# Layer 3's diagonal weights in early-free memory, its first image normalised on ScalarE, and the small group-norm operations of the scans moved off VectorE

## The chip, the cores and the metric

The kernel runs on one core of a Trainium2 chip. The metric is the device time of one execution in microseconds (us). The engines are called PE (TensorE, matmuls), DVE (VectorE), ACT (ScalarE), POOL (GpSimd) and SP (SyncE, which here only issues DMAs). Each engine has a program of its own and runs it in order. Semaphores let one engine wait for another.

## The reference

An input of 16 images with 192 channels of 64 x 64 pixels passes through four layers. Each one normalises its input by groups (32 groups of 6 channels), applies something and adds the result to its input:

```python
def _gn(v, G=32, eps=1e-5):
    g = v.reshape(B_, G, C_ // G, H_, W_)
    m = jnp.mean(g, axis=(2, 3, 4), keepdims=True)
    s = jnp.var(g, axis=(2, 3, 4), keepdims=True)
    return ((g - m) / jnp.sqrt(s + eps)).reshape(v.shape)

x = x + layer0(_gn(x))   # a small tanh network for each channel, a likelihood
x = x + layer1(_gn(x))   # a 192x960 product over each pixel and its 4 neighbours
x = x + layer2(_gn(x))   # selective scans over the image in 4 directions:
                         #   h = exp(d*A)*h + (d*u)*B ;  y = sum over 16 states of h*C
x = x + layer3(_gn(x))   # depthwise convolution (29 taps in all), 192x192 product,
                         #   batch norm over all images, clip to 0..6
```

## The kernel before

**Tiling.** Two images make a pair: 2 x 192 channels are NT = 3 tiles of 128 partitions (`j`) with 4096 pixels each. There are 8 pairs (`npair`, called "images" in the code). A pair goes through `front` (layers 0 and 1 and the projections of layer 2), `scans` (the recurrences of layer 2) and `layer3`. At the very end the batch norm of all pairs is applied.

**Scans.** `scans` runs 768 steps for a pair: 3 tiles x 4 directions x 4 stretches of 1024 pixels x 16 states. In one step DVE multiplies (`pbt<-du,pbt`, 1.21 us) and scans (`h<-dA,state,pbt`, 2.35 us), ACT computes `dA` and copies the last column into `state`, POOL multiplies `h` by `cb` (2.35 us), and PE spreads B over the partitions (`pbt`) and sums over states (`ysum`). SP loads a row of C for each step into `cb`, 512 KB. Every operation in here goes through `_Engines(tc, True)`: it is kept in the order of the program on its engine. Buffers run ahead: `dA` by three steps, `pbt` and `cb` by two, and `ysum` follows four steps behind (`LATE`) with eight buffers for `h`.

**The front of the next pair** is a generator that is advanced a little in each step of the scans, so layers 0 and 1 of pair i+1 run beside the scans of pair i. Only the front of the first pair runs alone, and there the operations are not kept in order. `group_norm` (line 357) is called three times in each front, and once more in the last 13 steps of the scans, for tiles 0 and 1 only (`gn0`, line 1048), because these two tiles are finished early. It aggregates the statistics (`mv`), copies the means, sums them over a group with small matmuls (`gn_sum`, a `yield` after each tile), forms `d2`, sums again, and takes the power -0.5 on POOL (`rstd`). All but the matmuls and the power are on DVE.

**Layer 3** (line 1107) is written without a kept order: a planner that orders instructions by the time at which it thinks them ready places them, some of them between the scans' own. Tile 0 (`xps[0]`) and tile 1 come back from DRAM, tile 2 is still in memory (`X`). Tile 0 is normalised on DVE in four pieces with `gm0, rstd0` from `gn0`. Then `group_norm` runs for all three tiles and tiles 1 and 2 are normalised. For each of 4 stretches `c` and each tile `j`, 8 taps are matmuls with diagonal matrices on PE (`l_p<-xp,diag`, line 1164), 8 taps are ACT products (`l_m`, line 1155) summed by POOL (`l_g`, line 1159, 7 additions), POOL's sum is added on PE with the identity (line 1176), and 13 taps run on DVE (line 1182). Then `pw` mixes the channels (`zp`, line 1196), ACT copies (`z`, line 1203) and DVE takes statistics (line 1204).

**Memory.** Pools lie one above the other, and the pools of layer 3 start at the place of those of `scans`. A tile in space that the scans used waits for the last reader there. In KB for each partition, counted from that place, the scans have `Xt` 0 to 16, `xc` to 20, eight `h` to 52, `dA` to 64, `cb` to 80, `state` to 80.2, and above that what the front uses. Layer 3 has its small tiles to 0.8, `z` to 8.8, `diag` 8.8 to 20.8, `pw` to 24.3, `l_g`, `l_m` and `l_y` to 68.3, an empty tile `gap` of `GAP` = 16 KB to 84.3, and then `xp0` and `xp1`, 19.1 KB each. `gap` puts the two images above the scans' own tiles: their space is free as soon as the front has ended.

Of the kernel before, what the change touches and what calls it, by code (L numbers as in the profile page):

```python
# [11 lines left out]
F32 = mybir.dt.float32  # L12
BF16 = mybir.dt.bfloat16
AF = mybir.ActivationFunctionType
ALU = mybir.AluOpType
# [7 lines left out]
P = 128  # L23
C = 192
NT = 3
# [24 lines left out]
PE_TAPS = 8  # L50
GP_TAPS = 8

GAP = 16


class _InOrder:


    def __init__(self, tc, engine):
        self._tc, self._engine = tc, engine  # L60
# [10 lines left out]
class _Engines:  # L71
# [3 lines left out]
    def __init__(self, tc, in_order):  # L75
        nc = tc.nc
        of = (lambda e: _InOrder(tc, e)) if in_order else (lambda e: e)
        self.pe, self.act, self.dve = of(nc.tensor), of(nc.scalar), of(nc.vector)
        self.gps, self.sp = of(nc.gpsimd), of(nc.sync)
        self._later = []  # L80
        self._in_order, self._table = in_order, None

    def later(self, call):

        if self._in_order:
            self._later.append(call)
        else:
            call()
# [4 lines left out]
        self._later.clear()  # L93

    def table(self, *names):
        if self._in_order and self._table not in names:
            self._table = names[0]
            self.act.preload_act_table_set(names[0])

# [7 lines left out]
def conv_preact_kernel(ctx: ExitStack, tc: tile.TileContext, a: dict):  # L107
    nc = tc.nc
    x_in = a["x"]
    out = a["out"]  # L110
    npair = x_in.shape[0]

    def row_tiles(ap):
        return ap.rearrange("(j p) l -> p j l", p=P)
# [4 lines left out]
    x3_d = dram.tile([npair, NT, P, S, S], F32, name="x3_d")  # L119
# [4 lines left out]
    diag_d = dram.tile([P, NT, PE_TAPS, P], F32, name="diag_d")  # L124
# [80 lines left out]
    with tc.tile_pool(name="prep", bufs=1) as prep, tc.tile_pool(  # L205
        name="prep_ps", bufs=2, space=PSUM
# [88 lines left out]
        for j in range(NT):  # L295
            diag = prep.tile([P, PE_TAPS, P], F32, name="diag", tag="diag", bufs=2)
# [43 lines left out]
    def normalise(eng, o, v, gm, rstd, j):  # L340
        eng.tensor_scalar(o, v, gm[:, j : j + 1], rstd[:, j : j + 1], ALU.subtract, ALU.mult)

    def on_scalar(E, o, v, less, rstd, j):

        E.act.activation(o, v, AF.Identity, bias=less[:, j : j + 1])
        E.act.activation(o, o, AF.Copy, scale=rstd[:, j : j + 1])
# [12 lines left out]
    def group_norm(E, st, stat, ps, gm, rstd, tiles=range(NT)):  # L359


        m = len(tiles)
        mv = stat.tile([P, NT, 2], F32, name="mv", tag="mv")
        mean = stat.tile([P, NT], F32, name="mean", tag="mean")
        d2 = stat.tile([P, NT], F32, name="d2", tag="d2")
        half = stat.tile([P, NT], F32, name="half", tag="half")
        E.dve.memset(half, -0.5)
        for j in tiles:
            E.dve.bn_aggr(mv[:, j, :], st[:, j, :, :].rearrange("p c s -> p (c s)"))
        mean, d2, half, mv = mean[:, :m], d2[:, :m], half[:, :m], mv[:, :m, :]  # L370
        gm, rstd = gm[:, :m], rstd[:, :m]
        E.dve.tensor_copy(mean, mv[:, :, 0])

        def mean_of(src):
            s = ps("gn_sum")
            for jo in tiles:
                into = [x for x in INTO[jo] if x[1] in tiles]
                for n, (b, ji) in enumerate(into):
                    E.pe.matmul(
                        s[:, jo : jo + 1],  # L380
                        grp[:, b, :],
                        src[:, ji : ji + 1],
                        start=(n == 0),
                        stop=(n == len(into) - 1),
                    )
                yield
            return s[:, :m]

        s = yield from mean_of(mean)
        E.dve.tensor_scalar(gm, s, 1.0 / 6.0, None, ALU.mult)  # L390
        E.dve.tensor_tensor(d2, mean, gm, ALU.subtract)
        E.dve.tensor_tensor(d2, d2, d2, ALU.mult)
        E.dve.tensor_tensor(d2, d2, mv[:, :, 1], ALU.add)
        s = yield from mean_of(d2)
        E.dve.tensor_scalar(d2, s, 1.0 / 6.0, 1e-5, ALU.mult, ALU.add)
        E.gps.tensor_tensor(rstd, d2, half, ALU.pow)


# [45 lines left out]
    def layer0(i, E, ps, deep, st, gm, rstd):  # L444
        with tc.tile_pool(name="l0w", bufs=1) as w_, tc.tile_pool(name="l0x", bufs=3) as xk, tc.tile_pool(
            name="l0", bufs=2
        ) as wk, tc.tile_pool(name="l0t", bufs=1) as tk:
            less = w_.tile([P, NT], F32, name="less")
            E.dve.tensor_scalar(less, gm, -1.0, None, ALU.mult)
            wm = w_.tile([P, NG, P + GR], F32, name="wms")  # L450
            wt = w_.tile([GR, NG, 2 * P], F32, name="wts")
            E.sp.dma_start(out=wm, in_=wm_d)
# [265 lines left out]
    def project(o, E, ps):  # L718

        with tc.tile_pool(name="pjw", bufs=1) as w_, tc.tile_pool(name="pjx", bufs=2) as xk:  # L720
            less = w_.tile([P, NT], F32, name="less")
            E.dve.tensor_scalar(less, o.gm, -1.0, None, ALU.mult)
            proj = w_.tile([P, NT, 2 * P + K * RD], F32, name="projs")
            E.sp.dma_start(out=proj, in_=a["proj"])
            xns = {}

            def load(c):
                if c < 8:
                    xns[c] = xk.tile([P, NT, 512], F32, name="pj_x")
                    for j in range(NT):  # L730
                        E.sp.dma_start(
                            out=xns[c][:, j, :],
                            in_=row_tiles(o.x2)[:, j, 512 * c : 512 * c + 512],
                        )

            load(0)
            yield
            for c in range(8):
                load(c + 1)
                xn = xns.pop(c)  # L740
                for j in range(NT):
                    on_scalar(E, xn[:, j, :], xn[:, j, :], less, o.rstd, j)
                    yield 0.36
                for to, d0, m in ((o.b, 0, P), (o.c, P, P), (o.dt, 2 * P, K * RD)):
                    p = ps("pj_p")[:m]
                    for j in range(NT):
# [103 lines left out]
    def scans(i, o, p3, st3, begun, nxt):  # L850

        E = _Engines(tc, True)
        with ExitStack() as es:

            def pool(name, bufs, **kw):
                return es.enter_context(tc.tile_pool(name=name, bufs=bufs, **kw))
# [8 lines left out]
            ps = Banks(pool("l2_ps", 1, space=PSUM), 2)  # L865
# [178 lines left out]
            fin = iter(())  # L1044
            gstep = iter(())

            gm0, rstd0 = (p3.tile([P, NT], F32, name=f"first{n}") for n in range(2))
            gn0 = group_norm(E, st3, p3, ps, gm0, rstd0, range(2))
            for s in range(total):
                t, n = divmod(s, N)  # L1050
                j, k, at, first = todo[t]
# [50 lines left out]
            E.between()  # L1102
            for _ in gn0:
                pass
            return gm0, rstd0

    def layer3(i, st3, gm0, rstd0, o_next):
        E = _Engines(tc, False)

        with tc.tile_pool(name="l3s", bufs=1) as stat, tc.tile_pool(name="l3z", bufs=2) as zk, tc.tile_pool(  # L1110
            name="l3w", bufs=1
        ) as w_, tc.tile_pool(name="l3", bufs=2) as wk, tc.tile_pool(name="l3gap", bufs=1) as gap, tc.tile_pool(
            name="l3x", bufs=1
        ) as xk, tc.tile_pool(name="l3_pt", bufs=2, space=PSUM) as pt, tc.tile_pool(
            name="l3_pz", bufs=4, space=PSUM
        ) as pz:
            gap.tile([P, GAP * 256], F32, name="gap")
            xps = [xk.tile([P, S, S], F32, name=f"xp{j}") for j in range(NT - 1)] + [X]
            for j in range(NT - 1):
                nc.sync.dma_start(out=xps[j], in_=x3_d[i, j])  # L1120
            for r in range(0, HW, 16):
                v = xps[0][:, 3 + r : 19 + r, inside]
                normalise(nc.vector, v, v, gm0, rstd0, 0)
            diag = w_.tile([P, NT, PE_TAPS, P], F32, name="diag")
            nc.sync.dma_start(out=diag, in_=diag_d)
            pw = load("pw", [P, len(BLOCKS), P], w_)
            nc.sync.dma_start(out=x3_d[i, NT - 1], in_=X)
            gm = stat.tile([P, NT], F32, name="gm")
# [4 lines left out]
            for j in range(1, NT):  # L1133
                v = xps[j][:, inside, inside]
# [10 lines left out]
            for c in range(4):  # L1145
# [3 lines left out]
                for j in range(NT):  # L1149

                    g = wk.tile([P, 1024], F32, name="l3_g")
                    for tap in TAPS[PE_TAPS:own]:
                        first = tap is TAPS[PE_TAPS]
# [6 lines left out]
                    ps = pt.tile([P, 1024], F32, name="l3_p")  # L1160
# [30 lines left out]
                for jo in range(NT):  # L1191
                    z = zk.tile([P, 1024], F32, name="z")
                    for h in range(2):
                        ps = pz.tile([P, 512], F32, name="zp", tag="ps")
# [11 lines left out]
                        out=row_tiles(z_d[i])[:, jo, 1024 * c : 1024 * c + 1024], in_=z  # L1206
# [24 lines left out]
    with tc.tile_pool(name="fin", bufs=1) as fin, tc.tile_pool(  # L1231
        name="fin_ps", bufs=1, space=PSUM
# [30 lines left out]
        ps = over_images(zs[:, :, :, 0])  # L1263
# [6 lines left out]
        ps = over_images(dev)  # L1270
# [127 lines left out]
```

## Time and profile before

| what | value |
|---|---|
| time, median of 3 runs (lowest to highest) | 27888.86 us (27888.48 to 27893.94) |
| the profiled execution's own time | 27887.51 us |
| its span, first to last instruction | 27885.6 us |
| mean granted TensorE clock | 0.912 |
| first front, alone | 0 to 1203 us |
| scans of a pair with a front beside them (7 of 8) | 2952 to 2960 us |
| scans of the last pair, no front | 2806 us |
| from the last scan of a pair to the first of the next (layer 3) | 341 to 342 us |
| after the last layer 3: batch norm and output | about 460 us |

The page of the profile gives busy shares over the whole span. Since the kernel has stages with different limits, it is read here stage by stage: the scans, and layer 3. In lines of the groups view, the number after the bar is the total busy time in us, then the mean of one instruction in ns, and after the second bar the idle time of its engine ahead of it with what ended it. In lines of the timeline the first two numbers are start and duration in us, and the bracket is the idle time of that engine just before.

### The profile page before, as it was taken

What the parts mean: (1) busy time and instruction counts of PE and PEld (TensorE: products, weight loads), DVE (VectorE), ACT (ScalarE), POOL (GpSimd) and SP (SyncE); (2) the same over time, 40 slices, a digit from 0 to 9 for tenths busy, and PEclk for the clock granted to TensorE, in tenths of its full rate; (3) what the DMA queues carried; (4) which work ended last, traced back from release to release, by engine and by line L of the source; (5) the groups of instructions that cost most, each with busy time, mean ns of one, the idle gap of its engine ahead of it and who ended that gap; (6) DMA issues with size and microseconds to landing.
All of it is one profiled execution on the core that took longest, in us unless ns stands there. A gap on an engine that the chain in (4) does not pass through costs nothing. (4 is left out here: it accounts for less than half of the span.)

```text
span 27885.6 us, 208702 instructions
## 1 busy us (share of the span) xinstructions
PE 23499.7 (84%) x57652; PEld 9648.3 (35%) x57652; DVE 24195.1 (87%) x15397; ACT 16075.9 (58%) x23023; POOL 20709.2 (74%) x10241
## 2 busy tenths in 40 slices
PE   8799978999789987999779997899878998776662
PEld 4343323333233332433334332333323333222221
DVE  0399988999899998999989998899989999899994
ACT  7388445874468643784548844587446854344442
POOL 2388877887778876888768877788777887677771
PEclk9899989999899988999889998999989999888886
DMA  4489764897468973888748976589747897367755
GB/s 101 136 225 230 212 206 141 225 223 220 152 191 226 223 223 117 224 227 219 215 124 229 225 213 193 152 227 224 221 134 208 226 222 222 110 189 193 198 164 241
DMA packets 1999218, 5471.76 MB, mean 196 GB/s; under 512 B 550440, under 2 KB 550664, under 8 KB 1977568
## 3 DMA queue, kind: packets, MB, share of 16 engines
q1 hardware_dynamic: 1773408, 4592.80, 55.6%
q0 software_dynamic: 221184, 805.40, 15.3%
q10 hardware_dynamic: 3456, 60.21, 0.5%
q8 instruction: 459, 7.52, 0.1%
q14 instruction: 711, 5.82, 0.1%
HBM read 3908.47 MB, written 340.96 MB: 152 GB/s over the span
## 5 line engine op out<-in xcount | busy, mean ns | idle before, releaser
L66 POOL TENSOR_TENSOR h<-h,cb 128x1024 f32<-128x1024 f32 x6144 | 14868.7, 2475 | 4513.4 <-ACT state L66 3628.4
L66 DVE TENSOR_TENSOR_SCAN h<-dA,state,pbt 128x1024 f32<-128x1024 f32 x4608 | 10809.3, 2346 | 722.2 <-ACT dA L66 120.6
L66 PE MATMUL ysum<-h,ident 128*128 128x512 f32 x18432 | 9462.4, 639 | 162.6 <-DMA h<-h 161.8
L66 DVE TENSOR_TENSOR pbt<-du,pbt 128x1024 f32<-128x1024 f32 x6144 | 7429.7, 1209 | 607.3 <-PE pbt L66 458.8
L66 ACT ACTIVATE dA<-delta,t_alog 128x1024 f32<-128x1024 f32 x6144 | 7034.1, 1146 | 6.5
L66 PEld LDWEIGHTS ysum<-h,ident 128*128 128x128 f32 x18432 | 3782.6, 206 | 4472.0 <-issue 3945.6
L66 ACT COPY state<-h 128x1 f32<-128x1 f32 x6144 | 1143.4, 186 | 6527.1 <-DVE h L66 6469.2
L66 PE MATMUL pbt<-bp,pick 96*128 96x512 bf16 x8192 | 2715.2, 416 | 2040.1 <-DVE h L66 1981.4
L66 DVE TENSOR_TENSOR_SCAN h<-dA,pbt 128x1024 f32<-128x1024 f32 x1536 | 3507.5, 2284 | 207.3 <-DMA h<-h 33.2
L66 PE MATMUL p<-t,wts 96*128 96x512 f32 x5376 | 2704.1, 601 | 129.9 <-ACT t L66 128.6
L66 PE MATMUL p<-m,wms 128*96 128x512 f32 (+1 forms) x5376 | 2646.4, 593 | 6.6 <-ACT lu L66 3.3
L66 PEld LDWEIGHTS <-pick 96*128 96x128 bf16 x8192 | 694.9, 101 | 4836.1 <-DVE h L66 3189.4
L66 ACT ACTIVATE t<-p,bias 96x512 f32<-96x512 f32 x2688 | 1803.6, 677 | 967.3 <-PE p L66 952.2
L1159 POOL TENSOR_TENSOR l_g<-l_g,l_m 128x1024 f32<-128x1024 f32 x672 | 1620.7, 2412 | 626.5 <-ACT l_g L1155 490.8
L66 PE MATMUL l_p<-l_xp,w1s 128*128 128x512 f32 x3920 | 1848.9, 600 | 9.1 <-POOL l_xp L66 9.0
L66 PE MATMUL pbt<-bp,pick_mix 96*128 96x512 bf16 x4096 | 1288.6, 397 | 548.9 <-DVE h L66 542.9
L66 POOL DMA_DIRECT2D h<-h x1536 | 1363.6, 888 | 495.1 <-POOL h L66 422.2
L66 PEld LDWEIGHTS p<-t,wts 96*128 96x128 f32 x5376 | 1009.7, 190 | 1277.2 <-issue 870.3
L66 ACT ACT_TABLE_LOAD x1082 | 1388.2, 1283 | 19.3
L1182 DVE SCALAR_TENSOR_TENSOR l_p<-xp,wc,l_p 128x1024 f32<-128x1024 f32 x768 | 990.4, 1290 | 246.9 <-PE l_p L1176 220.9
L66 PEld LDWEIGHTS p<-m,wms 128*96 128x96 f32 (+1 forms) x5376 | 944.1, 176 | 743.2 <-issue 359.1
L66 ACT ACTIVATE m<-m,bias,sp 96x512 f32<-96x512 f32 x1344 | 1078.0, 803 | 169.6 <-DMA m<-l_xn 164.6
(239 smaller groups left out, 18876.6 us busy)
## 6 DMA issues: line engine op xcount, KB each, us to landing
cb<-cp_d SPq DMA_DIRECT2D x2048, 512.0 KB
cb<-c_d SPq DMA_DIRECT2D x2048, 512.0 KB
h<-h POOLq DMA_DIRECT2D x1536, 512.0 KB, 7.0
cb<-cp_d SPq DMA_DIRECT2D x2048, 256.0 KB
cb<-c_d SPq DMA_DIRECT2D x2048, 256.0 KB
m<-l_xn SPq DMA_DIRECT2D x3072, 128.0 KB
bp<-bp_d SPq DMA_DIRECT2D x384, 192.0 KB
x_d<-X SPq DMA_DIRECT2D x24, 2450.0 KB
```

The lines of the kernel that those rows point to most:

```text
L66: return self._tc.keep_in_program_order(call(*args, **kw))
L1159: nc.gpsimd.tensor_tensor(g, g, m, ALU.add)
L1182: nc.vector.scalar_tensor_tensor(image(y if tap is TAPS[-1] else ps), window(j, 16 * c, 16, tap), factor(j, tap), image(ps), ALU.mult, ALU ...
```

## The change

Three things change.

1. `diag` moves from the pool `l3w` to the pool `l3x` of the two images, ahead of them, and `GAP` grows from 16 to 25. Its DMA is issued between those of `xp0` and `xp1`.
2. The first image of layer 3 (`xps[0]`) is normalised with `on_scalar` (two ACT operations for each of four pieces) in place of one DVE operation for each. `first_norm` hands over the negated mean for it (`less0`).
3. In a group norm whose operations are kept in order (`aside`), the copy of the means, the scaling of the first sum and that of the second go to ACT, and the constant, the three operations on `d2` and the added 1e-5 go to POOL. A `yield` is added ahead of the second sum. The negated means of layer 0 and of the projections (`less`) go to ACT.

```diff
-GAP = 16
+GAP = 25
@@ group_norm
-        E.dve.memset(half, -0.5)
+        aside = E.in_order
+        small = E.gps if aside else E.dve
+        small.memset(half, -0.5)
...
-        E.dve.tensor_copy(mean, mv[:, :, 0])
+        if aside:
+            E.act.copy(mean, mv[:, :, 0])
+        else:
+            E.dve.tensor_copy(mean, mv[:, :, 0])
...
         s = yield from mean_of(mean)
-        E.dve.tensor_scalar(gm, s, 1.0 / 6.0, None, ALU.mult)
-        E.dve.tensor_tensor(d2, mean, gm, ALU.subtract)
-        E.dve.tensor_tensor(d2, d2, d2, ALU.mult)
-        E.dve.tensor_tensor(d2, d2, mv[:, :, 1], ALU.add)
+        if aside:
+            E.act.activation(gm, s, AF.Copy, scale=1.0 / 6.0)
+        else:
+            E.dve.tensor_scalar(gm, s, 1.0 / 6.0, None, ALU.mult)
+        small.tensor_tensor(d2, mean, gm, ALU.subtract)
+        small.tensor_tensor(d2, d2, d2, ALU.mult)
+        small.tensor_tensor(d2, d2, mv[:, :, 1], ALU.add)
+        yield
         s = yield from mean_of(d2)
-        E.dve.tensor_scalar(d2, s, 1.0 / 6.0, 1e-5, ALU.mult, ALU.add)
+        if aside:
+            E.act.activation(d2, s, AF.Copy, scale=1.0 / 6.0)
+            E.gps.tensor_scalar(d2, d2, 1e-5, None, ALU.add)
+        else:
+            E.dve.tensor_scalar(d2, s, 1.0 / 6.0, 1e-5, ALU.mult, ALU.add)
         E.gps.tensor_tensor(rstd, d2, half, ALU.pow)
@@ layer0, and the same with o.gm in project
-            E.dve.tensor_scalar(less, gm, -1.0, None, ALU.mult)
+            E.act.activation(less, gm, AF.Copy, scale=-1.0)
@@ scans
-            gn0 = group_norm(E, st3, p3, ps, gm0, rstd0, range(2))
+            def first_norm():
+                yield from group_norm(E, st3, p3, ps, gm0, rstd0, range(2))
+                E.act.activation(less0[:, 0:1], gm0[:, 0:1], AF.Copy, scale=-1.0)
+
+            gn0 = first_norm()
@@ layer3
             gap.tile([P, GAP * 256], F32, name="gap")
+            diag = xk.tile([P, NT, PE_TAPS, P], F32, name="diag")
             xps = [xk.tile([P, S, S], F32, name=f"xp{j}") for j in range(NT - 1)] + [X]
-            for j in range(NT - 1):
-                nc.sync.dma_start(out=xps[j], in_=x3_d[i, j])
+            nc.sync.dma_start(out=xps[0], in_=x3_d[i, 0])
+            nc.sync.dma_start(out=diag, in_=diag_d)
+            nc.sync.dma_start(out=xps[1], in_=x3_d[i, 1])
             for r in range(0, HW, 16):
                 v = xps[0][:, 3 + r : 19 + r, inside]
-                normalise(nc.vector, v, v, gm0, rstd0, 0)
-            diag = w_.tile([P, NT, PE_TAPS, P], F32, name="diag")
-            nc.sync.dma_start(out=diag, in_=diag_d)
+                on_scalar(E, v, v, less0, rstd0, 0)
```

`on_scalar` was there before, for layer 0 and the projections:

```python
    def on_scalar(E, o, v, less, rstd, j):
        E.act.activation(o, v, AF.Identity, bias=less[:, j : j + 1])
        E.act.activation(o, o, AF.Copy, scale=rstd[:, j : j + 1])
```

More of the change, by code (lines that the diff above doesn't have):

```diff
@@ L80, in __init__ @@
         self._later = []
-        self._in_order, self._table = in_order, None
+        self.in_order, self._table = in_order, None
     def later(self, call):
-        if self._in_order:
+        if self.in_order:
             self._later.append(call)
@@ L95, in table @@
     def table(self, *names):
-        if self._in_order and self._table not in names:
+        if self.in_order and self._table not in names:
             self._table = names[0]
@@ L721, in project @@
             less = w_.tile([P, NT], F32, name="less")
-            E.dve.tensor_scalar(less, o.gm, -1.0, None, ALU.mult)
+            E.act.activation(less, o.gm, AF.Copy, scale=-1.0)
             proj = w_.tile([P, NT, 2 * P + K * RD], F32, name="projs")
@@ L1045, in scans @@
             gstep = iter(())
-            gm0, rstd0 = (p3.tile([P, NT], F32, name=f"first{n}") for n in range(2))
-            gn0 = group_norm(E, st3, p3, ps, gm0, rstd0, range(2))
+            gm0, rstd0, less0 = (p3.tile([P, NT], F32, name=f"first{n}") for n in range(3))
+            def first_norm():
+                yield from group_norm(E, st3, p3, ps, gm0, rstd0, range(2))
+                E.act.activation(less0[:, 0:1], gm0[:, 0:1], AF.Copy, scale=-1.0)
+            gn0 = first_norm()
             for s in range(total):
@@ L1104, in scans, with layer3 @@
                 pass
-            return gm0, rstd0
-    def layer3(i, st3, gm0, rstd0, o_next):
+            return less0, rstd0
+    def layer3(i, st3, less0, rstd0, o_next):
         E = _Engines(tc, False)
```

## The prediction

> **What bounds the kernel now.** First the windows view, over the first pair's scans and the start of its layer 3; then the groups of DVE.
>
> ```profile
> 1203.00:4157.00 2954.00, 2623.60 (x6544) 1082.08 (x6544) 2766.29 (x1696) 1869.89 (x2751) 2376.82 (x1188) 0.93 0.82 220
> 4164.25:4192.36 28.11, 7.42 (x30) 6.85 (x31) 20.45 (x22) 8.85 (x8) 21.89 (x8) 0.55 0.45 162
> 4192.36:4208.84 16.48, 16.48 (x40) 6.39 (x40) 4.74 (x2) 8.98 (x8) 11.37 (x5) 0.93 0.00 0
> ```
>
> After the length come PE, PEld, DVE, ACT, POOL. In the scans DVE is busy for 2766 of 2954 us, and much of its rest is a tenth of a us between dependent instructions: DVE bounds them. ACT has 1084 us free, POOL 577. Behind the last scan no engine is bound: PE works 7.4 of 28.1 us, then DVE 4.7 of 16.5.
>
> ```profile
> L66 DVE TENSOR_TENSOR_SCAN h<-dA,state,pbt 128x1024 f32<-128x1024 f32 x4608 | 10809.3, 2346 | 722.2 <-ACT dA L66 120.6 <-DMA h<-h 114.7 <-DVE pbt L66 87.3
> L341 DVE TENSOR_SCALAR xp<-xp,first,first 128x1024 f32<-128x1024 f32 x32 | 58.5, 1830 | 8.7 <-POOL first L66 8.7
> L66 DVE COPY mean<-mv 128x3 f32<-128x3 f32 (+1 forms) x29 | 56.5, 1949 | 1.0
> L66 DVE TENSOR_TENSOR d<-d,mv 128x3 f32<-128x3 f32 (+1 forms) x29 | 49.9, 1722 | 1.0
> L66 DVE TENSOR_TENSOR d<-d 128x3 f32<-128x3 f32 (+1 forms) x29 | 10.9, 376 | 1.0
> L66 DVE TENSOR_SCALAR d<-gn_sum 128x3 f32<-128x3 f32 (+1 forms) x29 | 4.4, 151 | 17.4 <-PE gn_sum L66 17.4
> ```
>
> A copy of three columns takes 1.95 us, about as long as a scan of 1024. The timeline says why:
>
> ```profile
> 4100.39 2.34 POOL L66 TENSOR_TENSOR h<-h,cb 128x1024 f32<-128x1024 f32 x1 [1.22 <-PE ysum L66]
> 4100.65 2.11 DVE L66 COPY mean<-mv 128x2 f32<-128x2 f32 x1
> 4110.22 2.35 POOL L66 TENSOR_TENSOR h<-h,cb 128x1024 f32<-128x1024 f32 x1 [1.23 <-ACT state L66]
> 4110.39 2.19 DVE L66 TENSOR_TENSOR d<-d,mv 128x2 f32<-128x2 f32 x1
> ```
>
> Both end with POOL's multiplication: DVE stands still for it, with the next product and scan behind. Last, the step from scans to layer 3, in the timeline:
>
> ```profile
> 4163.22 1.03 ACT L66 COPY X<-ysum 128x1024 f32<-128x1024 f32 x1 [5.94 <-PE ysum L66]
> 4166.50 21.49 POOL L1159 TENSOR_TENSOR l_g<-l_g,l_m 128x1024 f32<-128x1024 f32 x7 [6.80 <-ACT l_m L1155]
> 4176.22 0.32 SPq L1125 DMA_DIRECT2D diag<-diag_d  x1
> 4180.90 3.12 PE L379 MATMUL gn_sum<-mean,t_grp 128*128 128x1 f32 x14 [17.71 <-DVE mean L372]
> 4191.07 15.86 PE L1164 MATMUL l_p<-xp,diag 128*128 128x512 f32 x32
> 4208.84 17.23 DVE L1182 SCALAR_TENSOR_TENSOR l_p<-xp,wc,l_p 128x1024 f32<-128x1024 f32 x13 [11.71 <-PE l_p L1176]
> ```
>
> `diag` is loaded only when DVE has read `Xt` for the last time, PE's first product starts 27 us after the last scan's sum, and DVE then waits 11.7 us for it.
>
> **What the Trainium skill says.** "SBUF — State Buffer", § Who interferes with whom: a DVE copy or tensor_scalar in a two-port mode, and a tensor_tensor with two SBUF inputs, take the port pair that GpSimd uses, and who is second is blocked for the whole instruction of the other; ACT waits for nobody. The four lines above agree, and `d<-d` at 0.16 us between POOL's work shows the bare cost. "Perfetto Trace Analysis", § Optimizing Scalar/DVE Operations: with DVE saturated, move work to Scalar, or to GpSimd with the reservation of that port. "ScalarE: Activation LUTs", § Table sets: the hidden batching unit: copy and identity are in every set; so I count no table load (1.283 us each in this trace).
>
> **The change part by part.**
>
> *Small operations.* 29 group norms run in the scans (3 x 7 and 8). Gone from DVE: copies 56.5, `d<-d,mv` 49.9, `d<-d` 10.9, `d<-mean` 8.3 + 3.2 + 3.1, `gm` 2.0 + 1.1 + 1.0, `d<-gn_sum` 4.4, `less` 1.2 + 1.0: 142.6 us, and the 17.4 us that DVE waited for PE. The constant lies inside an aggregation: 0. Added to ACT: 3 or 4 operations like the state copy (0.186 us), into a row with 37% free. Added to POOL: 5; for its small tensor_tensor the trace has 0.2 us (96x6, in the preparation), so about 1 us for each norm, where POOL has 1.2 us free in each step of 3.57. Behind a late `d2` on POOL stands the next `h`; eight buffers and PE's four steps of distance cover it. Without this cover PE, and then `pbt`, would be late by that 1 us. The added `yield` costs the front a step, beside the scans: 0.
>
> *First image.* 32 tensor_scalars, 58.5 us, and 8.7 us of waiting for `rstd0` leave DVE. ACT gets 64 operations of 1.15 us (row `l_g<-xp,wc`, 1.152): 9.2 us for each pair, in the last 7 steps, where ACT works 17.8 of 74 us (windows view, 4090 to 4164). Behind them wait `state` (then POOL's `h`) and `dA`, three steps ahead. `xp0` is ready by about 20 us after `rstd0`, before X is copied.
>
> Sum of rows: 142.6 + 17.4 + 58.5 + 8.7 = 227 us. Successive DVE instructions overlap by some 0.07 us in the timeline (220 of them: 15 us). Check by steps, from one scan's start to the next in the timeline: around a front's norm, 6.2, 6.3 and some 3.9 us fall to 4.5 (the aggregations stay), 3.6 and 3.6, about 5 us for each of 21; around the last norm 6.25, 6.36, 6.43 and three of 5.46 fall to 4.25 and 3.6, 13.3 us for each of 8: 105 + 107 = 212 us. I take **-205**, bounds -225 and -150 (a quarter eaten by waits for PE's `pbt` and the h DMA, which end 459 and 148 us of DVE's idle time in the waits view).
>
> *Early `diag`.* Layer 3's pools lose 12 KB below `gap` and gap gains 9: `l_g` comes to 12.3 to 20.3 KB, on `Xt` and `xc`; `diag` to 81.3, above the scans' 80.2, `xp0` to 93.3. So `diag` is loaded with `xp0`, at 3773 us in the first pair, 400 us earlier. Its 1.5 MB pass SP beside the `cb` loads; the two images (4.9 MB) cost DVE 2.1 + 1.2 us there, waiting for the h DMA. Added: 1.5 us x 8 = **+12** (0 to +40).
>
> PE's 32 products of the first tile (14 to 16 us) can then run from 4163, in its idle 17.7 us ahead of `gn_sum`. DVE finds them done at 4197, when it has normalised tiles 1 and 2: up to 11.7 us for each pair. Against this, `l_g` can now be written only when `Xt` has been read (4176 before). But POOL then leaves the port alone: DVE's four additions took 1.94 us where POOL was idle and 2.9 beside it, so they and the norm end some 2 us earlier; POOL then ends its first sum near 4195, and starts the second, which waits for tile 1, near 4198 (4197 before). What is late next is POOL: a sum each 19.3 us (17.0 and 2.3 waiting), against DVE's 16.8 for a tile. In the chain of waits of the last layer 3, POOL's sums lead up to the first change of `c`; there `z` stands in ACT's program behind `l_m`, PE stands behind `z`, and POOL idles 13.4 us. PE and DVE some 10 us earlier let `z` come earlier and shorten that. I take 8 us x 8 = **-64**, bounds -184 and 0 short of the rival below.
>
> Sum: 27887.5 (the profiled execution's own time) - 205 - 64 + 12 = **27630 us**. The median of the runs lies 1.4 us above that execution; I leave this out.
>
> **Rivals.**
> A. Layer 3 gains nothing, because POOL's chain from tile 1 on is the bound (the chain view of the last layer 3 speaks for it; also the case if `diag` isn't early, for it has to pass SP). 27887.5 - 205 + 12 = 27694.
> B. The first change of `c` closes wholly: 10 + 13 us x 8 = -184: 27511. For it: the chain; against: the next changes of `c` keep stalls of their own.
> C. Slower. The order in layer 3 is a planner's. If it puts the power of the norm behind all seven additions of a first sum that starts 12 us later, `rstd` comes 8 us late, all tiles behind it, and if `z` then falls behind POOL at two more changes of `c`, 2 x 13.4: 35 us for each pair, 280 in all: 27694 + 280 = 27974. It decides from 24 us for each pair, which eats the 193. For it: the 13.4 us at the first change is such a stall now. Against: the norm stands ahead of the convolution in the program.
>
> **How the numbers follow.** Forecast 0.55, A 0.26, B 0.10, C 0.09. The range of the likeliest is 27560 to 27690; A lies at its edge, B just inside the lower end that I give, C outside: **27500 to 27770**. 0.2% (56 us) is what a measurement of this kernel can tell from no change. Forecast, B and most of A are faster by more: 0.87; within: 0.05 (A with the bound of -150); slower: 0.08.
>
> **What would show it.** Scans of 2927 us with a front and 2793 without; `mean` on ACT at 0.2 us; no step above 5 us among the last 13 of the scans; `diag` issued near `xp0`; the first `l_p` of a pair within 5 us of the last `ysum`; the 11.7 us before DVE's first tap gone; 330 us between the scans in place of 341. I am wrong in the first part if POOL or PE make DVE wait in those steps, in the second if POOL's second sum starts later than 33 us behind the X copy.

## The result and the profile after

| what | before | after |
|---|---|---|
| median (lowest to highest), 4 runs each on the same chip | 27889.76 us (27888.48 to 27893.94) | 27646.29 us (27639.74 to 27651.77) |
| the profiled execution's own time | 27887.51 us | 27649.24 us |
| mean granted TensorE clock | 0.912 | 0.918 |

The ratio of after to before is 0.9912, with a 95% interval of 0.9895 to 0.993. The forecast was 27630 us. It is 16 us off, but two of its terms were off by more than that, in opposite directions. The trace, cut into stages at the first and last scan of each pair, shows it:

| stage, us | before | after | difference |
|---|---|---|---|
| first front, alone | 1203.3 | 1203.5 | +0.2 |
| scans of all 8 pairs | 23498.2 | 23259.1 | -239.1 |
| the 7 gaps between the scans of two pairs (layer 3) | 2390.2 | 2391.0 | +0.8 |
| from the last scan to the end | 793.8 | 793.9 | +0.1 |

All of the gain is in the scans. Layer 3, for which 64 us were forecast, gained nothing: 341.5 us for each pair before, 341.6 after.

The windows view of the kernel after, over the stretches that answer to those of before (columns: length, then busy us and count of PE, PEld, DVE, ACT, POOL, then clock, DMA share, GB/s):

```profile
1203.00:4120.00 2917.00, 2601.85 (x6544) 1071.65 (x6544) 2732.94 (x1662) 1882.11 (x2775) 2379.84 (x1208) 0.94 0.83 223
4126.71:4151.02 24.31, 19.56 (x56) 11.45 (x55) 16.64 (x23) 7.81 (x7) 7.96 (x5) 0.78 0.33 123
4151.02:4168.01 16.99, 8.81 (x18) 2.28 (x18) 8.80 (x3) 6.95 (x6) 16.68 (x6) 0.71 0.00 0
```

The first line is 37 us shorter, and DVE has 33 us less work in it. In the second, the way to the normalisation of tiles 1 and 2 is 3.8 us shorter and PE works 19.6 us of it instead of 7.4: the diagonal products did move forward. In the third DVE is busy for 8.80 us where it was 4.74, with the same two normalisations in it, and POOL is busy all the time.

The groups of the kernel after show where the small operations went, and at what price (total us, then mean ns):

```profile
L66 DVE TENSOR_TENSOR_SCAN h<-dA,state,pbt 128x1024 f32<-128x1024 f32 x4608 | 10809.2, 2346 | 736.2 <-ACT dA L66 106.0 <-DMA h<-h 99.4 <-DVE pbt L66 83.8
L66 POOL TENSOR_SCALAR d<-d 128x3 f32<-128x3 f32 x21 | 12.2, 581 | 0.0
L66 POOL TENSOR_TENSOR d<-d,mv 128x3 f32<-128x3 f32 x21 | 4.1, 197 | 1.6
L66 ACT COPY mean<-mv 128x3 f32<-128x3 f32 x21 | 3.7, 177 | 0.0
L345 ACT ACTIVATE xp<-xp,first 128x1024 f32<-128x1024 f32 x32 | 35.6, 1158 | 0.3
L346 ACT ACTIVATE xp<-xp,first 128x1024 f32<-128x1024 f32 x32 | 37.1, 1158 | 0.0
```

The copy of the means that took 1.95 us on DVE takes 0.177 us on ACT. The timeline of the last steps of the first pair's scans:

```profile
4076.12 0.57 DVE L66 BATCH_NORM_AGGREGATE mv<-st 128x2 f32<-128x48 f32 x2
4076.62 1.21 DVE L66 TENSOR_TENSOR pbt<-du,pbt 128x1024 f32<-128x1024 f32 x1
4077.93 2.35 DVE L66 TENSOR_TENSOR_SCAN h<-dA,state,pbt 128x1024 f32<-128x1024 f32 x1
...
4087.89 0.50 POOL L66 TENSOR_TENSOR d<-mean,first 128x2 f32<-128x2 f32 x1
4088.47 0.20 POOL L66 TENSOR_TENSOR d<-d 128x2 f32<-128x2 f32 x1
4088.75 0.20 POOL L66 TENSOR_TENSOR d<-d,mv 128x2 f32<-128x2 f32 x1
```

DVE has only the aggregation between two steps. The step with it takes 4.07 us from scan to scan and the others 3.57 to 3.67, where six steps of before took 5.46 to 6.43.

Now the step from the scans to layer 3, in the timeline of the kernel after:

```profile
4125.45 11.45 PE L1183 MATMUL l_p<-xp,diag 128*128 128x512 f32 x26
4125.65 1.03 ACT L66 COPY X<-ysum 128x1024 f32<-128x1024 f32 x1 [5.50 <-PE ysum L66]
4136.65 1.17 ACT L1174 ACTIVATE l_g<-xp,wc 128x1024 f32<-128x1024 f32 x1 [9.98 <-DVE X L66]
4139.01 7.21 POOL L1178 TENSOR_TENSOR l_g<-l_g,l_m 128x1024 f32<-128x1024 f32 x3 [16.44 <-DVE st L66]
4150.11 0.88 POOL L410 TENSOR_TENSOR rstd<-d,half 128x3 f32<-128x3 f32 x1 [3.89 <-DVE d L409]
4151.02 4.43 DVE L341 TENSOR_SCALAR xp<-xp,gm,rstd 128x4096 f32<-128x4096 f32 x1 [0.99 <-POOL rstd L410]
4155.37 4.44 DVE L341 TENSOR_SCALAR X<-X,gm,rstd 128x4096 f32<-128x4096 f32 x1
4164.49 3.46 PE L1195 MATMUL l_p<-l_g,ident 64*64 64x512 f32 x8 [6.12 <-POOL l_g L1178]
4168.01 11.89 DVE L1201 SCALAR_TENSOR_TENSOR l_p<-xp,wc,l_p 128x1024 f32<-128x1024 f32 x9 [8.19 <-PE l_p L1195]
```

PE's first product starts 0.2 us ahead of the X copy. But ACT's `l_g` waits 9.98 us for DVE's last reading of `Xt` (the name behind the arrow is `X`, the sum that reads it), POOL's first sum begins 12.3 us behind the X copy's end, is held up for `rstd` after three of its additions, and the rest of it runs beside DVE's two normalisations. These take 4.43 and 4.44 us, where they took 2.4 before, and POOL's last four additions of that sum take 13.5 us (4150.97 to 4164.49), where the first three took 7.2. DVE then still waits, 8.19 us, for PE's addition of POOL's sum.

### The profile page after: what moved, and what is told of

Its sections match the earlier page's. It is cut to its first block, busy times and chain, and to the rows that moved or that the text cites. A ratio compares the mean times of both kernels' runs of the same rounds, so it can differ in the third digit from the quotient of the medians.

```text
span 27647.5 us, 208708 instructions
## 1 busy us (share of the span) xinstructions
PE 23437.4 (85%) x57652; PEld 9614.6 (35%) x57652; DVE 23966.9 (87%) x15146; ACT 16170.9 (58%) x23198; POOL 20728.4 (75%) x10386
## 5 line engine op out<-in xcount | busy, mean ns | idle before, releaser
L66 DVE TENSOR_TENSOR pbt<-du,pbt 128x1024 f32<-128x1024 f32 x6144 | 7427.4, 1209 | 592.2 <-PE pbt L66 444.7
```

The lines of the kernel that those rows point to most:

```text
L66: return self._tc.keep_in_program_order(call(*args, **kw))
```

## The experiments

Two things were open: whether the parts of the gain add up, and what holds layer 3. Each kernel below has one time, beside the kernel before on the same chip; the last but one was timed repeatedly. Differences in the total below some 56 us are not read as such. The stage sums from the traces are finer, with a spread of up to 33 us in the sum of the eight scans between kernels that do the same in them, and of 1 to 2 us in one layer 3.

**The parts one at a time.** Small operations alone: `diag` and the first image as before.

```diff
-            diag = xk.tile([P, NT, PE_TAPS, P], F32, name="diag")
...
-                on_scalar(E, v, v, less0, rstd0, 0)
+                normalise(nc.vector, v, v, gm0, rstd0, 0)
+            diag = w_.tile([P, NT, PE_TAPS, P], F32, name="diag")
```

> Part 3 alone: small operations of the norms off VectorE, the rest as before. If a saved VectorE instruction counts at its full length in the scans (theory), the rows of before give 144 us: about 27746 us, and layer 3 stays at 341 us between the scans. If the two added yields of a front, which shift layers 0 and 1 against the 16 states of a stretch, bring the rest of what the scans gained (rival), it is 27715 us and the steps of layer 1 far from any norm are shorter.

First image alone:

```diff
-        aside = E.in_order
+        aside = False
...
-        yield
...
+            diag = w_.tile([P, NT, PE_TAPS, P], F32, name="diag")
+            nc.sync.dma_start(out=diag, in_=diag_d)
```

> Part 2 alone: the first image of layer 3 normalised on ScalarE. Theory: the rows of before, 58.5 + 8.7 us, all of it: about 27823 us, the steps of 5.46 us near the end of the scans gone, layer 3 unchanged at 341 us. Rival (ScalarE's extra 9.2 us for each pair hold up state and dA): less than 30 us, with steps above 4 us where the pieces lie.

Early `diag` alone:

```diff
-        aside = E.in_order
+        aside = False
...
-                on_scalar(E, v, v, less0, rstd0, 0)
+                normalise(nc.vector, v, v, gm0, rstd0, 0)
```

> Part 1 alone: diag in early-free memory. Theory (the head's gain is eaten by l_g, which now lies on Xt): 27890 us within 20, layer 3 at 341 us, PE's first product right behind the last sum, but POOL's first addition 19 us behind the last scan in place of 9.4. Rival (early diag is worth something, hidden in the whole change by another part): 27830 us or less.

| kernel | time, us | before beside it | difference | scans, 8 pairs | layer 3, a pair |
|---|---|---|---|---|---|
| small operations alone | 27722.26 | 27907.4 | -185 | 23332.6 | 341.3 |
| first image alone | 27838.49 | 27907.4 | -69 | 23453.3 | 340.9 |
| early `diag` alone | 27921.02 | 27907.4 | +14 | 23531.7 | 341.5 |

The first two sum to -254 us, against -243 for the whole change: as far as one time each can tell, they add, and the third adds nothing. The small operations gave 41 us more than the theory had for them. That is less than one time can tell, but it is the rival's number; the run with the `yield` alone, below, tests that rival. The early `diag` does in its own run what it does in the change (first product 6.0 us behind the last scan instead of 34), and layer 3 stays where it was. Its +14 us are below what one time can tell. The traces tell more: the two images, and here `diag` between them, are issued in the steps 667 to 676 of the first seven pairs, and the steps 660 to 720 of these take 1545.2 us in sum with the early `diag` alone and 1544.6 before. No cost of its DMA shows there.

**The space of `l_g`.** An empty tile of 12 KB below `l_g` puts it back where it lay before, above `Xt`; `gap` gives the 12 KB up, so `diag` and the images stay where the change has them.

```diff
-            gap.tile([P, GAP * 256], F32, name="gap")
+            low.tile([P, 12 * 256], F32, name="low")
+            gap.tile([P, (GAP - 12) * 256], F32, name="gap")
```

> The whole change, with an empty tile of 12 KB below l_g and gap 12 KB smaller, so that l_g, l_m and l_y lie where they lay before and diag stays early. Theory (l_g's wait for Xt eats the gain of the head): POOL's first addition 9.4 us behind the last scan, VectorE's first tap near 38 to 42 us (48.1 with the change), layer 3 at 331 to 337 us, in all 27565 to 27610 us. Rival (the order of z and l_m on ScalarE at the change of c sets layer 3, whatever the head): first tap earlier too, but layer 3 stays at 341 us: 27646 us.

27633.38 us (before beside it 27907.4: -274), layer 3 338.6 us. The tile does what it should: POOL's first addition comes 9.0 us behind the last scan instead of 19.1, and the first of the two normalisations is back at 2.41 us and the second at 3.49. DVE's first tap comes 8.7 us earlier than in the kernel after, and yet layer 3 is only 3.0 us shorter, less than the theory asked for (331 to 337 us). So the new wait on `Xt` is real and costs 3 us for each pair; it isn't what ate the rest.

**The `yield` alone**, in the kernel before:

```diff
         E.dve.tensor_tensor(d2, d2, mv[:, :, 1], ALU.add)
+        yield
         s = yield from mean_of(d2)
```

> The kernel before with the added yield alone, nothing moved off VectorE. The whole change shortened the stretch of steps 480 to 576 (layer 1, no norm in it) by 10.9 us for each pair and lengthened 48 to 96 by 4.8 and 624 to 672 by 3.7. Theory (the yields shift the front against the states): the same signs and sizes here within 2 us, the scans of a pair 0 to 5 us shorter, in all 27850 to 27900 us. Rival (it is the freed VectorE that shortens them): no stretch moves by more than 2 us.

27901.22 us, before beside it 27897.6: no difference. The three stretches did move as expected (by -9.7, +4.9 and +4.6 us for each pair), so it is the `yield` that shifts them, but the eight scans in sum didn't get shorter (23512.0 us against 23498.2): the `yield` by itself brings no gain, against the rival of the first run. Two things inside moved. The normalisation of the next tile's `xn` on DVE, 4096 columns, stood behind a run of POOL's in the kernel before; with the front one step later it doesn't. The timelines of DVE and POOL of the kernel before,

```profile
3097.69 8.48 DVE L66 TENSOR_SCALAR xn<-xn,gm,rstd 128x4096 f32<-128x4096 f32 x1
...
3096.78 7.23 POOL L66 TENSOR_TENSOR h<-h,cb 128x1024 f32<-128x1024 f32 x3
```

and of the kernel after, at the same step of the scans:

```profile
3091.88 2.39 DVE L66 TENSOR_SCALAR xn<-xn,gm,rstd 128x4096 f32<-128x4096 f32 x1
...
3090.50 4.33 POOL L66 TENSOR_SCALAR l_xp<-l_xp,fgm,frstd 128x640 f32<-128x640 f32 x1
```

8.48 us against 2.39 for the same instruction. Over all pairs the `xn` normalisations inside the scans fall from 106.3 to 68.5 us with the `yield` alone, and to 73.2 us in the kernel after. In the run with the `yield` alone this comes back as waiting: DVE's idle time that ends with POOL's `h` or `X` rises from 61.3 to 106.2 us (waits view). It does the same in the kernel after (102.5 us).

**The order of DVE's taps.** On top of `l_g` off `Xt`, the taps are kept in the order of the program instead of the planner's. In the planner's order, with `l_g` off `Xt`, three taps of tile 1 stand ahead of tile 0's last one, and the first of them waits 6.6 us for POOL's second sum.

```diff
+            V = _InOrder(tc, nc.vector)
...
-                        nc.vector.scalar_tensor_tensor(
+                        V.scalar_tensor_tensor(
```

> l_g off Xt as in e4_l_g_off_Xt, and the taps on VectorE kept in the order of the program. Theory (in the planner's order, taps of tile 1 stand ahead of the last taps of tile 0 and wait for POOL's sum, so that the early start is lost): tile 0's l_y ends near 50 to 55 us behind the X copy's end (63 in e4), tile 2's first tap by 74 us (82), layer 3 at 325 to 333 us (338), in all 27540 to 27600 us. Rival (POOL's sums at 19.3 us set it whatever VectorE's order): tile 0 earlier, but layer 3 within 2 us of 338.

27619.17 us (before 27897.6: -278), layer 3 336.6 us. Tile 2's first tap now comes 11.1 us earlier than in the kernel before, which is what the forecast asked for ("PE and DVE some 10 us earlier"), but the first tap of `c` = 1 only 4.5 us earlier, and layer 3 misses the theory's 325 to 333 us. Timelines of DVE, PE and ACT of this run:

```profile
4200.51 2.61 DVE L66 SCALAR_TENSOR_TENSOR l_p<-X,wc,l_p 128x1024 f32<-128x1024 f32 x2
4216.96 0.69 DVE L1225 BATCH_NORM_STATS2 zst<-z 128x6 f32<-128x512 f32 x1 [13.85 <-ACT z L1224]
...
4199.87 7.13 PE L1217 MATMUL zp<-l_y,t_pw 128*128 128x512 f32 x16
4216.98 2.08 PE L1217 MATMUL zp<-l_y,t_pw 128*128 128x512 f32 x2 [9.98 <-ACT z L1224]
...
4215.31 1.15 ACT L1176 ACTIVATE l_g<-xp,wc 128x1024 f32<-128x1024 f32 x1
4216.37 0.56 ACT L1224 COPY z<-zp 128x512 f32<-128x512 f32 x1
```

PE has the first products for `z` ready at 4207.0 and waits 9.98 us for the first copy of `z`; DVE waits 13.85 us, in the middle of tile 2's taps, for the statistics of `z`. ACT copies the first `z` only at 4216.37, right behind an `l_g` of the next stretch, and this one stands behind a row of `l_m` that follow POOL's additions at 2.43 us each. Whatever PE and DVE gained ends there.

**A third buffer for `l_g`**, with the planner's order and with the order kept. (Each `l_g` is one sum of POOL's; with two, ACT can begin the sum after next only when PE has added one.)

```diff
-                    g = wk.tile([P, 1024], F32, name="l3_g")
+                    g = wk.tile([P, 1024], F32, name="l3_g", bufs=3)
```

> l_g off Xt, and three buffers for l_g in place of two. Theory (at each change of c POOL idles 13 us because ScalarE's next l_g needs a buffer that PE reads late): those waits of POOL fall under 5 us, the distance between first taps of c=2 and c=3 falls from 68.4 to 60 to 65 us, layer 3 at 310 to 328 us. Rival (PE is at its limit there, busy 63 of 68 us): POOL idles elsewhere and layer 3 stays above 333 us.

> Both: taps in order and three buffers for l_g, l_g off Xt. Theory: the gains add, layer 3 at 300 to 322 us, in all 27430 to 27560 us. Rival (PE's limit): no shorter than the shorter of e7_taps_in_order and e8_three_l_g by more than 2 us for each pair.

27763.85 and 27747.74 us (before 27897.6), layer 3 355.3 and 353.7 us: 17 us longer for each pair than with two buffers. The theory missed: POOL's idle time at the change of `c`, 13.58 us in the kernel after, is not there for want of a buffer. It stays. The timelines of POOL, PE and ACT of the first of the two show this, and why it got worse:

```profile
4270.56 16.99 POOL L1179 TENSOR_TENSOR l_g<-l_g,l_m 128x1024 f32<-128x1024 f32 x7 [13.43 <-ACT l_g L1175]
...
4240.62 2.07 PE L1216 MATMUL zp<-l_y,t_pw 128*128 128x512 f32 x2 [16.71 <-ACT z L1223]
...
4238.94 1.15 ACT L1175 ACTIVATE l_g<-X,wc 128x1024 f32<-128x1024 f32 x1
4240.00 0.56 ACT L1223 COPY z<-zp 128x512 f32<-128x512 f32 x1
```

ACT runs one more sum ahead, of tile 2 instead of tile 1, and comes to `z` that much later.

**`z` copied on DVE.** Taps in order and `l_g` off `Xt`, with two buffers and with three:

```diff
-                        nc.scalar.copy(z[:, 512 * h : 512 * h + 512], ps)
+                        nc.vector.tensor_copy(z[:, 512 * h : 512 * h + 512], ps)
```

> The order of VectorE's taps is kept as written, l_g is off Xt, and the copies of z out of PSUM go from ScalarE to VectorE (24 of about 0.6 us per pair). Theory: the change of c is late because the z copies stand in ScalarE's program behind l_m that wait for POOL's sums. Then the first tap of c=1 comes by about 108 us behind the last scan (122.7 in the run with ordered taps alone), layer 3 takes 325 us or less (336 there), 27530 us or less in all. Rival: TensorE and POOL set the pace of layer 3 whatever the change of c does: layer 3 within 3 us of 336, 27600 to 27640 us. A third way: VectorE's extra copies lengthen it, 340 us or more.

> As the run with z on VectorE, with three l_g buffers in place of two. With two buffers and z on ScalarE the third buffer cost 17 us per pair, by the theory since ScalarE then ran further ahead with l_g and l_m and came to z later. With z off ScalarE the theory expects no loss from the third buffer: layer 3 at or below that of the run with z on VectorE (325 us or less). Rival, the third buffer harms for another reason (ScalarE and POOL ahead of VectorE in the planner's order): layer 3 at 345 us or more, 27700 us or more in all.

With two buffers: 27464.56 us (before 27913.02: -448), layer 3 318.4 us, the first tap of `c` = 1 at 104.4 us. That is what the theory asked for, and the gain is net of DVE's 24 further copies for each pair (0.68 us each). With three: 27574.13 us (-339), layer 3 335.3 us. Here the theory missed: no loss was expected from the third buffer, and it costs 17 us as it did before. The first tap of `c` = 1 does come at 104.4 us there too; the loss is at `c` = 2. In the timelines of PE, of the run with two buffers first, then of the run with three:

```profile
4297.17 12.73 PE L1185 MATMUL l_p<-xp,diag 128*128 128x512 f32 x22 [23.90 <-ACT delta L846]
```

```profile
4317.84 12.76 PE L1185 MATMUL l_p<-xp,diag 128*128 128x512 f32 x22 [40.83 <-ACT delta L846]
```

`delta` is the start of the next pair's scans, which the program calls ahead of the third stretch. It takes an `l_p` bank, and its one operation on ACT stands behind `l_m` that wait for POOL, as `z` did. The kernel before has that wait too, at 10.46 us.

**The next pair's start called earlier**, on top of `z` on DVE with two buffers:

```diff
-                if c == 2 and o_next is not None:
+                if c == 0 and o_next is not None:
```

> As the run with z on VectorE, with the start of the next pair's scans (its first delta, with a table load on ScalarE, and a buffer of l_p) called ahead of the first stretch c instead of ahead of the third. Theory: in the run with z on VectorE, TensorE's l_p of c=2 waits 23.9 us for this delta, which stands in ScalarE's program behind l_m that wait for POOL; the last pair, with no next pair, needs 281 us from its last scan to its last tap where the others need 309. Then the early call gives layer 3 about 290 us for each pair (318 there) and 27464 - 28 x 7 = 27270 us in all. Rival: the delta finds no earlier place on ScalarE, or it delays the first sum of POOL, which then delays all the rest: layer 3 at 310 us or more, 27400 us or more.

27292.3 us (27286.08 to 27297.96, 4 runs) against 27911.98 us (27895.62 to 27919.69, 7 runs): ratio 0.978, interval 0.9764 to 0.9797. Layer 3 takes 294.5 us, where the theory had about 290. In the timeline of ACT, `delta` now comes while ACT has little to do:

```profile
4131.74 1.17 ACT L1176 ACTIVATE l_g<-xp,wc 128x1024 f32<-128x1024 f32 x1
4132.93 1.28 ACT L846 ACT_TABLE_LOAD   x1
4134.23 1.11 ACT L846 ACTIVATE delta<-l_p,t_dtb 128x1024 f32<-128x1024 f32 x1
```

It does delay POOL's first sum, as the rival said (its first addition comes 13.3 us behind the last scan instead of 9.0), and `c` = 1 starts 4.4 us later than with the late call; but `c` = 2 starts 24 us earlier. This kernel is faster than both the kernel before and the kernel after. The 13 us at the changes of `c` are gone from POOL's timeline; ahead of the sums shown it idles 2.34 us:

```profile
4259.21 17.01 POOL L1180 TENSOR_TENSOR l_g<-l_g,l_m 128x1024 f32<-128x1024 f32 x7 [2.33 <-ACT l_g L1176]
4278.56 16.99 POOL L1180 TENSOR_TENSOR l_g<-l_g,l_m 128x1024 f32<-128x1024 f32 x7 [2.34 <-ACT l_g L1176]
4297.88 16.98 POOL L1180 TENSOR_TENSOR l_g<-l_g,l_m 128x1024 f32<-128x1024 f32 x7 [2.34 <-ACT l_g L1176]
```

A stretch takes about 61 us now (170.1 less 108.8 in the table below). In the windows view of 61 us PE is busy for nearly all of it:

```profile
4235.00:4296.00 61.00, 59.57 (x148) 24.38 (x147) 56.92 (x52) 29.14 (x26) 52.04 (x23) 1.00 0.06 24
```

**`z` on DVE alone**, in the changed kernel, with its `l_g` on `Xt` and the planner's order (the edit is the one above):

> The changed kernel with one edit: z is copied on VectorE instead of ScalarE; l_g stays on the space of Xt and the planner orders the taps. Theory: of what held layer 3 at 341 us in the changed kernel, the place of z in ScalarE's program is the larger part. Then c=1 starts by about 112 us behind the last scan (127 in the changed kernel), layer 3 takes 322 to 330 us, and 27500 to 27560 us in all. Rival: the later first sum of POOL and the planner's order of the taps hold the change of c as much, so that z alone gives little: c=1 at 122 us or later, layer 3 at 336 us or more.

27554.38 us (before 27911.98: -358), layer 3 328.9 us: moving the copies of `z` gives 12.7 us for each pair where the early `diag` gave none. The first tap of `c` = 1 came at 119.8 us, where the theory said 112. That the planner's order and the late first sum keep the rest is likely, but no run shows it.

The milestones of the first pair's layer 3 side by side, in us behind the end of its last scan (the last line is the mean of seven gaps):

| | before | after | `l_g` off `Xt` | and taps in order | and `z` on DVE | and next pair early |
|---|---|---|---|---|---|---|
| PE, first `l_p` | 34.0 | 5.5 | 5.5 | 5.5 | 5.5 | 6.7 |
| POOL, second sum | 40.1 | 44.5 | 39.8 | 39.8 | 39.8 | 40.3 |
| DVE, first tap of tile 0 | 51.8 | 48.1 | 39.4 | 39.7 | 39.7 | 42.8 |
| DVE, first tap of tile 1 | 67.7 | 63.5 | 62.5 | 59.8 | 59.3 | 62.9 |
| DVE, end of tile 0's last tap | 70.2 | 73.1 | 69.7 | 56.9 | 56.8 | 63.0 |
| DVE, first tap of tile 2 | 88.0 | 91.8 | 88.4 | 76.9 | 76.4 | 80.8 |
| DVE, first tap of `c` = 1 | 127.2 | 127.0 | 123.9 | 122.7 | 104.4 | 108.8 |
| DVE, first tap of `c` = 2 | 208.9 | 208.7 | 205.5 | 204.7 | 194.1 | 170.1 |
| layer 3 | 341.5 | 341.6 | 338.6 | 336.6 | 318.4 | 294.5 |

Read the first two columns side by side: 28.5 us of gain at the first line are 3.7 us at DVE's first tap and 4.2 at the first tap of tile 1. But that tap stands ahead of the last ones of tile 0 in DVE's program, waits 3.5 us for POOL's second sum, and so tile 0 ends 2.9 us later than before. PE's products for tile 2 wait for that end, tile 2 starts 3.8 us later, and from `c` = 1 on the two kernels are level.

## Why the prediction came out as it did

**The scans: right in mechanism, 34 us too small.** -205 was taken and -239 measured, outside the lower bound of -225. Against the mean of the three traces that have neither part (23514 us: before, early `diag` alone, `yield` alone) the small operations alone give -181, the first image alone -61, and the nine traces with both, 23259 to 23274 us, -248 on average. The bounding fact, that DVE is the bound and every removed instruction counts at nearly its full length, held; so did the costs put at nothing on ACT and POOL. The mis-sized term is the reduction from the rows' 227 us to 205: the waits for PE's `pbt` and for the DMA of `h`, of which the forecast feared more, didn't grow (458.8 to 444.7 us and 147.9 to 118.8). In the scans DVE's busy time, overlaps counted once, fell by 225.3 us and its idle time by 13.9. The removed rows make 201 us, and `xn`, which I hadn't counted, 33; overlaps eat some 9 of these. Nor had I counted that waits for POOL's `h` and `X` rose by 41 (the `yield` makes this rise and the fall of `xn`, as its own run shows, and nets to nothing), and that DVE's waits for the DMA of `h` fell by 29 us. This last goes with the small operations: all ten traces with them have 107 to 130 us, the four without 144 to 171. Why, no run took apart.

**Layer 3: the step that failed.** "PE and DVE some 10 us earlier let `z` come earlier and shorten that. I take 8 us x 8 = -64." It measured 0. Two steps fail one after the other.

First, PE and DVE were not 10 us earlier in the changed kernel. "POOL then ends its first sum near 4195" put that end 31 us behind the X copy; it came 38 us behind it (4164.5 less 4126.7). The wait on `Xt` was in the sum. Not in it were the pause for `rstd`, which the planner placed behind the third addition (4.8 us with the power itself), and that the rest of the sum would run beside the normalisations of tiles 1 and 2, where both were slower. The Trainium skill, "SBUF — State Buffer", § Who interferes with whom, has this (the two share a port pair, and the second is blocked for the other's instruction), and I used it for the scans; the trace agrees, with 4.43 us for DVE's normalisation beside POOL and 2.41 without. I applied it to DVE's additions, which did get faster, and not to what took their place beside POOL. My own sign of failure, "POOL's second sum starts later than 33 us behind the X copy", came true: 37.7 us. The order of DVE's taps, which let tile 0 end later than before, stood in no term either.

Second, and larger: even 11 us earlier, `z` doesn't follow. The run with taps in order has the forecast's premise and gives 4.9 us for each pair against the kernel before: 2.9 with the wait on `Xt` gone, 2.0 more with the order. I had read the chain rightly (`z` stands in ACT's program behind `l_m`, PE behind `z`, POOL idles) and drew the wrong conclusion from it: a copy that stands behind `l_m` is timed by POOL's row of sums, not by PE and DVE. The early `diag` doesn't move the end of that row: POOL's fourth sum ended 95.7 us behind the last scan before and 95.3 after, and the first `z` followed at 97.9 and 97.5. The Trainium skill, "PSUM — Partial Sum Buffer", § Engine vs sequencer instructions, calls ScalarE's queue strictly first in, first out, and the trace agrees: with PE's products done at 4207.0, `z` came at 4216.37, right behind the `l_g` at 4215.31. Taking `z` out of ACT's program is what shortened it, by 18.2 us for each pair, and by 12.7 in the changed kernel without any other edit.

**Rival A had the outcome, not quite the cause.** Layer 3 gained nothing, as it said. Its reason, that POOL's chain is the bound, is half of it: POOL sets the time of ACT's program, but POOL itself idles 13.6 us at the change of `c`, and a third buffer doesn't cure that. A sum of POOL every 19.3 us, A's bound, is kept through all the changes of `c` only in the run with the next pair's start called early. As the traces show it, the bound was a ring: POOL's additions, `l_m`, `z` on ACT, PE's next `l_p`, its addition of `l_g`, and ACT's next `l_g` for POOL. Rival B's 23 us for each pair (10 + 13) came only with `z` on DVE, taps in order and `l_g` off `Xt` (341.5 to 318.4). Rival C did not come: the power of the norm went behind the third addition, not behind the seventh.

**The DMA of `diag`.** +12 was taken. It was issued between the two images, 39 us behind the first in the first pair:

```profile
3772.01 0.43 SPq L1139 DMA_DIRECT2D xp<-x_d  x1
3810.60 0.43 SPq L1140 DMA_DIRECT2D diag<-diag_d  x1
```

No cost shows: in the run with the early `diag` alone, the steps around its load took 0.6 us more than before, in sum over seven pairs.

**The total.** 27630 + 64 (layer 3) - 12 (`diag`) - 34 (scans) = 27648 us, against the profiled execution's 27649.24. The total came within 0.1% by luck: a gain that was too small in the scans and one that didn't come in layer 3 nearly cancelled.

## What to carry to other kernels

When an engine's program is in order, ask of each instruction on the path not only what it waits for but what stands ahead of it: a short copy behind a row of operations that follow another engine is timed by that engine, and feeding it earlier gains nothing. Work that is brought forward gains only as far as the first such place, so follow it past the wait that it removes to the end of the stage, and move that copy instead.

A tile that is moved in memory moves the tiles around it, and each new neighbour in space can be a wait, and each new neighbour in time on a shared port a slower instruction. Where one engine was the bound over a whole stage, in contrast, removed instructions were worth nearly their full length here.

## What the runs showed of the hardware

The same DVE instruction, a tensor_scalar over 4096 columns, took 2.41 us with POOL quiet, 4.43 us beside a row of POOL's additions, and 8.48 us behind a run of three of its multiplications of `h`. One step more or less in the program of the front decided between 8.48 and 2.39 us.

Small operations on POOL are not all alike: with three columns a tensor_tensor took 0.20 us, the first of a row 0.36 to 0.50, a tensor_scalar 0.58 (0.23 with two columns), the power 0.72 to 0.89. I had put them at 0.2 each; beside POOL's free time in a step it made no difference here.

PE's 32 products of a tile took 16.65 us after it had waited 9.82 us and 14.15 us when they followed its other work directly (timelines of the kernel after, and of the run with taps in order):

```profile
4193.20 16.65 PE L1183 MATMUL l_p<-X,diag 128*128 128x512 f32 x32 [9.82 <-DVE l_y L1201]
```

```profile
4162.73 14.15 PE L1185 MATMUL l_p<-xp,diag 128*128 128x512 f32 x32
```

In the kernel after, all seven rows of 32 behind such a wait (9.8 us, one for each pair but the last) took 15.52 to 16.68 us, and all 21 that followed other work directly took 14.15. So the wait cost PE 1.4 to 2.5 us more than its length. The windows view of just the two rows shown, of the kernel after and of the run with taps in order, has the granted clock in its third column from the right:

```profile
4193.20:4209.85 16.65, 16.65 (x34) 6.93 (x36) 11.37 (x9) 9.19 (x8) 16.18 (x8) 0.85 0.00 1
```

```profile
4162.73:4176.88 14.15, 14.15 (x34) 5.94 (x32) 13.80 (x12) 9.53 (x9) 13.12 (x6) 1.00 0.00 0
```

14.15 us at a clock of 0.85 are 16.65 us: the lower clock accounts for all of it. The Trainium skill, "TensorE: Matmul & The Clock Gate", § Part 1: The HAM clock gate (the "warmup" mystery), says that PE falls to half its clock after about 3.4 us without work and needs about as long at work to come back. The traces agree in kind, not in the figure: in the kernel after, a wait of 2.67 us was enough in 18 of 21 cases (15.79 to 15.81 us for the row behind it, at a clock of 0.89; the other three took 14.12 us at 1.00). No run here varied the length of a wait alone.
